# Cross-attention on one Trainium2 core: eleven block products of 64 rows in place of twelve for the folded key weights

## The chip, the cores and the metric

The kernel runs on one core of one Trainium2 chip. The metric is the device time of one execution in microseconds. A core has PE (TensorE, matrix products into the banks of PSUM), DVE (VectorE), ACT (ScalarE), POOL (GpSimd) and SP (SyncE, which here issues the transfers). Each engine works through its own queue in order; semaphores order work between engines.

## The reference

Multi-head cross-attention, all in float32, with 16 batches of 256 queries (256 wide), 77 keys (192 wide) and 8 heads of width 256:

```python
Q = (img_embed @ Wq).reshape(B, -1, H, D).transpose(0, 2, 1, 3)
K = (sent_embed @ Wk).reshape(B, -1, H, D).transpose(0, 2, 1, 3)
V = (sent_embed @ Wv).reshape(B, -1, H, D).transpose(0, 2, 1, 3)
score = jnp.einsum('bhqd,bhkd->bhqk', Q, K) / math.sqrt(D)
score = jnp.where(mask, score, -jnp.inf)
attn = jax.nn.softmax(score, axis=-1)
ctx = jnp.einsum('bhqk,bhkd->bqhd', attn, V).reshape(B, -1, H * D)
out = ctx @ Wo + img_embed
mu = jnp.mean(out, axis=-1, keepdims=True)
var = jnp.var(out, axis=-1, keepdims=True)
return (out - mu) * jax.lax.rsqrt(var + EPS) * gamma + beta
```

## The kernel before

The weights are folded. For each head, G = Wk Wq^T / sqrt(D) is a 192 x 256 matrix, kept as gA (the first 128 of its 192 rows, per head) and gB (the other 64; two heads share the partitions). With the transposed keys c, kept as cA (128 rows) and cB (64 rows, there twice), A = G^T c is a 256 x 77 matrix for each batch and head, and the scores are x A. In the same way U = Wv Wo (uA, uB) gives vw = c U, and the output is p vw.

The prologue builds G and U, and A of group 0 (a group is four batches). After it a loop runs over b from -1 to 14. One pass does, in the order of the code:

- `scores` of the two query tiles of batch b+1 on PE (L303, into ps), `shift` of them on DVE (L320: adds the mask and takes the largest score of a row), `exponential` on ACT (L340), `weigh` (the reciprocal on DVE, L355, then the product p on POOL, L361), and `turn` (the transpose pT of p on DVE, L371);
- `prepare_vw` on PE (L227 for the 128 rows, L238 for the 64; bank pv, copied to vw by ACT at L963), and `differences` on POOL (L414, ts);
- `prepare_a`: A of two heads of a later group, a quarter of a group's A, as 308 columns (four batches of 77 keys) for each head and half of the 256 rows: L193 for the 128 rows with 32 columns of weights each, L205 for the 64 rows; four banks pa, copied to a by ACT (L963);
- `seven` on PE (L450: p vw of batch b by seven block products; banks pm and po), `sums` on POOL (L431 to L434, ss, for the next `seven`), `add_product` on DVE (L498, po into xg), `add_seven` on POOL (L484);
- the normalisation of batch b-1: `finish` (L506, L509), `spread` on ACT (L527, L528), `normalise` on DVE (L548, L577); `turn_last` (L293) and `transpose_x` (L165) on DVE.

Every second pass (b = -1, 1, 3, 5, ...) is a long one: it holds `prepare_vw` for two batches and two quarters of A. The passes between are short and hold neither. Until b = 7 the quarters are those of groups 1, 2 and the first half of group 3.

All PSUM tiles come from one pool of 8 banks, taken in turn: a tile waits until the tile eight places before it has been read by all its readers. A long and a short pass take 24 banks. The order on each engine is the order in which the code records the operations; nothing reorders them. Transfers of x, c and the outputs go through SP's queue.

Of the kernel before, what the change touches and what calls it, by code (L numbers as in the profile page):

```python
# [27 lines left out]
def kernel(  # L28
# [52 lines left out]
    gB = const.tile([P, NF, DI], F32, tag="gB", name="gB")  # L81

# [85 lines left out]
    def prepare_a(g, places, lo=0, hi=GB, rest_first=False):  # L168
# [16 lines left out]
        def cols(dc, i):  # L185
            return slice((2 * i + dc) * BK, (2 * i + dc + 1) * BK)
# [29 lines left out]
        return part_A, part_B, copies  # L216

# [382 lines left out]
    with tc.tile_pool(name="wonce", bufs=1) as wp:  # L600
# [33 lines left out]
        def turn_rest():  # L634
            nc.vector.transpose(flat(cA)[:, rest], flat(cA)[:, rest])
            nc.gpsimd.tensor_copy(cRA, cA[:, :, KM:])

        def turn_rest_last():
            nc.vector.transpose(flat(cB)[LB:, rest], flat(cB)[LB:, rest])
            nc.gpsimd.tensor_copy(flat(cB)[:LB, rest], flat(cB)[LB:, rest])  # L640
            nc.gpsimd.tensor_copy(cRB, cB[:, :, KM:])
# [186 lines left out]
        def g_of_pair(a):  # L828

            banks = [ps_mm.tile([P, DI], F32, tag="mm", name=f"pgb_{a}_{e}") for e in range(2)]  # L830
            for n in range(4):
                for i in range(2):
                    for e in range(2):
                        nc.tensor.matmul(  # L834
                            banks[e][half(i)],
                            kT_blk[a][half(e), n, half(i)],
                            qT_blk[a][half(e), n],
                            start=(n == 0),
                            stop=(n == 3),
                        )  # L840
            for e, o in enumerate(banks):
                nc.scalar.mul(gA[:, 2 * a + e], o, D ** -0.5)
# [42 lines left out]
        for a in range(1, NF):  # L885
# [7 lines left out]
            a_of_pairs(a, rest_first=True)  # L893
        load_x(0)
# [10 lines left out]
        for j in range(NF // 2):  # L905
# [13 lines left out]
            for e, pw in enumerate(  # L919
# [3 lines left out]
                for i in range(2):  # L923
                    for k in range(2):
# [24 lines left out]

    def work_of(b, rest_first=False):  # L950
        g, n = b // GB + 1, b % GB
        work = [prepare_vw(b, rest_first)]
        if g < NG - 1 or g == NG - 1 and n < NF // 2:
            work.append(prepare_a(g, (n,), rest_first=rest_first))
        elif b <= NS:
# [21 lines left out]
    for b in range(-1, B - 1):  # L977
# [17 lines left out]
        works = work_of(b + 1) if alone or n % 2 == 0 else []  # L995
        for part_A, _, _ in works:
            part_A()
        for _, part_B, _ in works:
            part_B()
# [23 lines left out]
        ahead = works and not alone  # L1023
        if old and not ahead:
            spread(old[0], old[-1] + 1)
        if ahead:
            copy_out(works)
            if old:
                spread(old[0], old[-1] + 1)
            works = work_of(b + 2, rest_first=True)  # L1030
            for _, part_B, _ in works:
                part_B()
            for part_A, _, _ in works:
                part_A()
        copy_out(works)
# [4 lines left out]
        if b < NS:  # L1040
            if now:
                seven(b)
            if old:
                invert(old[0], old[-1] + 1)
                normalise(old[0])
            for t in new:
                turn(t)
            if b < 0:
                for t in range(QT, GT, 2):
                    transpose_x(t)  # L1050
                bias_of(GB, B)
            if alone or ahead:
# [65 lines left out]
```

## Time and profile before

| | us |
|---|---|
| median of 3 runs | 270.32 (270.11 to 270.44) |
| the profiled execution | 269.95 |
| its span | 268.2 |
| PE busy | 262.5 (98%) |
| DVE busy | 185.9 (69%) |
| POOL busy | 173.2 (65%) |
| ACT busy | 157.6 (59%) |
| A by L193 and L205 (PE, all groups) | 36.6 and 20.4 |

The span is the profiler's time from the first to the last instruction; the device time has 1.75 us around it. The clock granted to PE is 1.00 throughout. A row of a group gives line, engine, operation, out<-in, shapes and count, then the busy time, the mean duration of one in ns, and the idle time of the engine just before such instructions with what ended it. A row of the timeline gives start, length, engine, line and operation; idle time before it stands in brackets. A float32 matmul leaves two records on PE.

### The profile page before, as it was taken

To read this page: it belongs to the slowest core of one execution; us is meant where nothing else is said; L and a number is where in the kernel's file an instruction comes from. 1 tells how busy PE (TensorE), PEld (TensorE's weight loads), DVE (VectorE), ACT (ScalarE), POOL (GpSimd) and SP (SyncE) were. 2 spreads that over 40 slices of the span, in tenths; PEclk is the share of its full clock that TensorE was granted. 3 is DMA by queue.
4 is the path that set the end of the run, shared out by engine and by line. 5 is a ranking of instruction groups with operands and counts; after the bars stand their busy time and mean duration, and the time that the engine had idled before them with its cause. 6 is when DMAs were issued, how large, how long until landed. Compare 5 with 4: busy or idle time off the path is not lost.

```text
span 268.2 us, 14455 instructions
## 1 busy us (share of the span) xinstructions
PE 262.5 (98%) x6090; PEld 191.8 (72%) x6090; DVE 185.9 (69%) x808; ACT 157.6 (59%) x667; POOL 173.2 (65%) x240
## 2 busy tenths in 40 slices
PE   8999999999999999999999999999999999999992
PEld 8566578944984699459944995499669957985662
DVE  1555967493583868665886379647977887799785
ACT  3243336536857565955596468737775595636772
POOL 1042005728399739994799669965998799585452
PEclk9999999999999999999999999999999999999999
DMA  6989987901500130232012401340034010100112
GB/s 190 217 199 228 334 138 142 311 21 34 129 7 2 46 80 2 63 111 71 5 43 90 112 5 43 91 113 2 6 120 122 4 45 2 44 22 22 46 40 80
DMA packets 41696, 22.69 MB, mean 85 GB/s; under 512 B 24144, under 2 KB 40608, under 8 KB 41632
## 3 DMA queue, kind: packets, MB, share of 16 engines
q1 hardware_dynamic: 41248, 20.98, 30.1%
q0 software_dynamic: 384, 0.79, 1.3%
q8 instruction: 48, 0.79, 1.3%
q14 instruction: 16, 0.13, 0.2%
HBM read 17.57 MB, written 4.19 MB: 81 GB/s over the span
## 4 chain that ended last, share of the span: by engine, by line
PE 98%; DVE 1%; issue 0%; DVEq 0%
PE ps L303 25%; PE pa L193 13%; PE pv L227 11%; PE po L450 11%; PE pm L450 8%; PE pa L205 6%; PE pv L238 6%; PE po L383 4%; PE pu L773 3%; PE pr L263 2%; PE pgb L834 2%; PE pw L787 1%; PE idle L703 1%; PE pr L274 1%; PE phb L850 1%; PE po L399 1%
## 5 line engine op out<-in xcount | busy, mean ns | idle before, releaser
L340 ACT ACTIVATE s<-s,top 128x77 f32<-128x77 f32 x256 | 85.3, 346 | 44.2 <-DVE top L320 37.9
L303 PE MATMUL ps<-a,xT 128*32 128x154 f32 x2048 | 69.9, 294 | 0.0
L303 PEld LDWEIGHTS ps<-a,xT 128*32 128x32 f32 x2048 | 66.2, 110 | 1.2 <-issue 0.4
L361 POOL TENSOR_TENSOR p<-s,rden 128x512 f32<-128x512 f32 x64 | 47.5, 768 | 29.5 <-DVE rden L355 29.4
L320 DVE CUSTOM_DVE_ANT_0 s<-ps,bias 128x77 f32<-128x77 f32 x256 | 43.5, 232 | 14.3 <-PE ps L303 14.3
L340 ACT ACTIVATION_READ_ACCUMULATOR s<-s,top 128x1 f32 x224 | 42.0, 187 | 0.0
L193 PE MATMUL pa<-cA,gA 128*32 128x308 f32 (+1 forms) x576 | 36.6, 395 | 0.0
L193 PEld LDWEIGHTS pa<-cA,gA 128*32 128x32 f32 x576 | 18.3, 110 | 21.0 <-issue 7.0
L484 POOL TENSOR_TENSOR xg<-xg,m 128x256 f32<-128x256 f32 x39 | 28.7, 736 | 6.6 <-DVE xg L498 4.5
L577 DVE SCALAR_TENSOR_TENSOR xg<-xg,rstd,bet 128x256 f32<-128x256 f32 x27 | 22.9, 847 | 14.0 <-ACT rstd L528 12.6
L227 PE MATMUL pv<-uA,cA 128*32 128x512 f32 x256 | 30.6, 595 | 0.0
L371 DVE STREAM_TRANSPOSE pT<-p 128x640 f32<-128x640 f32 x32 | 25.5, 821 | 3.4 <-POOL p L361 3.3
L414 POOL TENSOR_TENSOR ts<-vw 128x768 f32<-128x768 f32 x13 | 24.0, 1848 | 5.9 <-ACT vw L963 5.9
L963 ACT COPY vw<-pv 128x512 f32<-128x512 f32 x32 | 17.8, 584 | 14.8 <-PE pv L227 8.3
L498 DVE TENSOR_TENSOR xg<-po,xg 128x256 f32<-128x256 f32 x31 | 11.5, 405 | 13.8 <-PE po L450 13.3
L320 DVE DVE_READ_ACCUMULATOR2_ANT top<- 128x1 f32 x256 | 20.8, 81 | 0.0
L205 PE MATMUL pa<-cB,gB 64*32 64x308 f32 (+2 forms) x512 | 20.4, 387 | 0.0
L963 ACT COPY a<-pa 128x308 f32<-128x308 f32 (+1 forms) x56 | 18.9, 395 | 1.9 <-PE pa L193 0.4
L205 PEld LDWEIGHTS pa<-cB,gB 64*32 64x32 f32 (+1 forms) x512 | 11.0, 110 | 11.4 <-issue 6.2
L548 DVE SCALAR_TENSOR_TENSOR xg<-xg,mv,gam 128x256 f32<-128x256 f32 x30 | 17.6, 588 | 0.1
L238 PE MATMUL pv<-uB,cB 64*32 64x512 f32 x256 | 17.3, 597 | 0.0
L227 PEld LDWEIGHTS pv<-uA,cA 128*32 128x32 f32 x256 | 7.5, 109 | 12.8 <-issue 9.9
(119 smaller groups left out, 404.1 us busy)
## 6 DMA issues: line engine op xcount, KB each, us to landing
xg<-in_x_dram SPq DMA_DIRECT2D x8, 512.0 KB, 4.4
xT<-in_x_dram SPq DMA_DIRECT2D x56, 64.0 KB, 2.6
out_dram<-xg SPq DMA_DIRECT2D x11, 256.0 KB, 2.2
wo<-in_L_xattn_Wo_dram SPq DMA_DIRECT2D x4, 512.0 KB, 7.8
wq_blk<-in_L_xattn_Wq_dram SPq DMA_DIRECT2D x12, 128.0 KB, 4.3
out_dram<-xg SPq DMA_DIRECT2D x10, 128.0 KB, 1.9
wk_blk<-in_L_xattn_Wk_dram SPq DMA_DIRECT2D x12, 96.0 KB, 3.6
wvT<-in_L_xattn_Wv_dram POOLq DMA_DIRECT2D x8, 96.0 KB, 6.6
```

The source lines that it names most:

```text
L193: nc.tensor.matmul(flat(o[i * BK : (i + 1) * BK]), gA[:, h, cols(dc, i)], flat(cA[:, batches, :]), start=not rest_first and n in opening, ...
L205: nc.tensor.matmul(flat(banks[j + k][i * BK : (i + wide) * BK]), gB[half(k), h // 2, dc * P + i * BK : dc * P + (i + wide) * BK], flat(cB[ ...
L227: nc.tensor.matmul(pv[k][i * BK : (i + 1) * BK], cA[:, b, k * BK : (k + 1) * BK], uA[:, parts, :, i], start=not rest_first, stop=rest_first,)
L238: nc.tensor.matmul(pv[k][i * BK : (i + 1) * BK], cB[half(k), b, k * BK : (k + 1) * BK], uB[half(k), parts, :, i], start=rest_first, stop=n ...
L303: nc.tensor.matmul(ps[m // 2][i * BK : (i + 1) * BK, m % 2 * 2 * S2 : (m % 2 + 1) * 2 * S2], xT_of[t // PT][:, j * NM + m, dc], flat(a_of[ ...
L320: nc.vector.tensor_tensor_reduce(s[:, h], ps[a][:, k * S2 : (k + 1) * S2], bias[:, b, :], scale=-1.0, scalar=FAR, op0=ALU.add, op1=ALU.min ...
L340: nc.scalar.activation(s[:, h], s[:, h], AF.Exp, bias=top[:, one], scale=-1.0, accum_out=den[:, one] if summed_by_act(t) else None,)
L361: nc.gpsimd.tensor_tensor(part, e_mh[:, :, :, keys], rden_mh.unsqueeze(3).to_broadcast(list(part.shape)), ALU.mult,)
L371: nc.vector.transpose(pT_of[t].rearrange("p n m q -> p m n q"), p.rearrange("p m (n k) -> p m n k", k=BK),)
L450: nc.tensor.matmul(out[i * BK : (i + 1) * BK], weight[:, i], moving, start=first and n == 0, stop=final and n == len(terms) - 1,)
L484: nc.gpsimd.tensor_tensor(to, to, what, ALU.add)
L963: nc.scalar.copy(dst, src)
```

## The change

For groups 1, 2 and the first half of group 3 the three block rows of G (64 rows each) and the two halves of a group's batches (154 columns) are combined as in a fast matrix product. For one head, A's two halves of 128 rows and the two halves of the batches are four outputs, each a sum of three block products: twelve. Five products (`middle`) and six (`outer`) of sums of the blocks now give them: eleven.

On PE, `prepare_fast(g, u)` takes the place of a quarter of `prepare_a`. Its matmuls contract 64 rows into 64 rows of PSUM. `products` walks eleven pairs; a pair has one product on partitions 0 to 63 and one on 64 to 127, each in two halves of 64 output rows, so four matmuls of 154 columns. The two heads use four banks: mids and ends for each. The first product of `middle` goes to a bank alone and is copied to a by ScalarE (L369 of the changed kernel), before the same bank is started anew by that head's second product of `middle`, in the fifth pair for the first head and in the eighth for the second.

On DVE, `put_together(e)` makes a of one head from its two banks and that copy by four additions (L372).

The operands need sums: `sums_of_g`, `last_sums_of_g` (gS, and gC, a copy of half of gB on the other partitions), `sums_of_c` (cT) and `differences_of_c` (cD). They run once, in the prologue, on POOL and, as copies, on ACT. The copies of `turn_rest` and `turn_rest_last` go from POOL to ACT. gA's columns are stored in another order, so that 64 of them are adjacent.

In the long passes up to b = 7 the vw products of both batches now come first, then the two calls of `products`, and the sums of DVE stand between and behind the two transposes of p. The core of the diff:

```diff
+    add, subtract = (
+        partial(nc.gpsimd.tensor_tensor, op=op) for op in (ALU.add, ALU.subtract)
+    )
...
+    def sums_of_g():
+        for parts, sums, e, own, other in parts_of_g():
+            nc.scalar.copy(sums[own, 0, e], parts[other, 1, e])
+            nc.scalar.copy(gC[own], gB[other, :, P:])
+        for parts, sums, e, own, other in parts_of_g():
+            s1, s2, s3 = (sums[own, n, e] for n in range(3))
+            add(s1, s1, parts[own, 1, e])
+            subtract(s2, s1, parts[own, 0, e])
+            subtract(s3, parts[own, 0, e], parts[own, 1, e])
...
+    def sums_of_c(lo, hi):
+        xs, ys = halves_of(cA, lo, hi)
+        t1, t2, t3, t4 = (cT[:, n, lo - 1 : hi - 1] for n in range(4))
+        subtract(t1, ys, xs)
+        for own, other in ((low, high), (high, low)):
+            nc.gpsimd.tensor_copy(t2[own], ys[other])
+        subtract(t3, t2, ys)
+        subtract(t2, t2, t1)
+        for own, other in ((low, high), (high, low)):
+            nc.gpsimd.tensor_copy(t4[own], t2[other])
+        subtract(t4, xs, t4)
...
+        def middle(e):
+            h, own = heads[e], (high, low)[e]
+            return [
+                ((mids[e], 2), from_g(own, h, 0), c_of(cA, own, xs)),
+                ((mids[e], 0), from_s(own, 0, h), t_of(own, 0)),
+                ((mids[e], 2), from_s(own, 1, h), t_of(own, 1)),
+                ((mids[e], 1), from_s(own, 2, h), t_of(own, 2)),
+                ((mids[e], 1), lambda i: gC[own, u, half(i)], c_of(cB, own, ys)),
+            ]
...
+        def pairs():
+            o, m = outer(0), middle(1)
+            ones = o[:2] + m[:1] + o[2:] + m[1:]
+            o, m = outer(1), middle(0)
+            return list(zip(ones, m[:1] + o[:3] + m[1:] + o[3:]))
+
+        def products():
...
+                for i in range(2):
+                    for ((bank, n), weight, moving), (start, stop, _) in zip(pair, flags):
+                        nc.tensor.matmul(
+                            bank[half(i), n], weight(i), moving, start=start, stop=stop,
+                        )
+                for ((bank, n), _, _), (_, _, one) in zip(pair, flags):
+                    if one:
+                        nc.scalar.copy(blocks[lone[id(bank)]][:, 0], by_batch(bank)[:, n])
...
+        def put_together(e):
+            mid, end, of = by_batch(mids[e]), by_batch(ends[e]), blocks[e]
+            plus(of[:, 3], mid[:, 2], of[:, 0])
+            plus(of[:, 1:3], mid[:, 0:2], of[:, 3:4].to_broadcast([P, 2, HB, S2]))
+            plus(of[:, 3], mid[:, 0], of[:, 2])
+            plus(of[:, 0:3], end, of[:, 0:3])
...
         def turn_rest():
             nc.vector.transpose(flat(cA)[:, rest], flat(cA)[:, rest])
-            nc.gpsimd.tensor_copy(cRA, cA[:, :, KM:])
+            nc.scalar.copy(cRA, cA[:, :, KM:])
 
         def turn_rest_last():
             nc.vector.transpose(flat(cB)[LB:, rest], flat(cB)[LB:, rest])
-            nc.gpsimd.tensor_copy(flat(cB)[:LB, rest], flat(cB)[LB:, rest])
-            nc.gpsimd.tensor_copy(cRB, cB[:, :, KM:])
+            nc.scalar.copy(flat(cB)[:LB, rest], flat(cB)[LB:, rest])
+            nc.scalar.copy(cRB, cB[:, :, KM:])
...
+        if quick:
+            works += work_of(b + 2)
+            for part_A, *_ in works:
+                part_A()
+            for _, part_B, _ in works:
+                part_B()
+            copy_out(works[:1])
+            products, put_together = prepare_fast(g, n)
+            products()
+            copy_out(works[1:])
...
+            next_products, next_together = prepare_fast(g, n + 1)
+            next_products()
+            if old:
+                spread(old[0], old[-1] + 1)
...
+            if quick:
+                if b >= 0:
+                    turn(new[0])
+                put_together(0)
+                put_together(1)
+                if b >= 0:
+                    turn(new[1])
             if old:
                 invert(old[0], old[-1] + 1)
                 normalise(old[0])
-            for t in new:
-                turn(t)
...
+            if quick:
+                next_together(0)
+                next_together(1)
```

How this moves the queues is shown for the long pass b = 3, whose tiles of queries are 8 and 9. DVE's queue from the second reciprocal to the next shift, before (pT is the transpose of p; xg holds the rows to be normalised; po is the result of `seven`):

```order
L355 RECIPROCAL rden_9_1933<-den_9_1921 128x8
L548 SCALAR_TENSOR_TENSOR xg_1_518<-xg_1_518,mv_0_1346,gam_69 128x256
L577 SCALAR_TENSOR_TENSOR xg_1_518<-xg_1_518,rstd_4_1944,bet_90 128x256
L371 STREAM_TRANSPOSE pT_8_2086<-p_0_85 128x4x5x32
L371 STREAM_TRANSPOSE pT_9_2088<-p_1_86 128x4x5x32
L165 STREAM_TRANSPOSE xT_3_1441<-xT_3_1441 128x512 x2
L548 SCALAR_TENSOR_TENSOR xg_1_518<-xg_1_518,mv_0_1346,gam_69 128x256
L577 SCALAR_TENSOR_TENSOR xg_1_518<-xg_1_518,rstd_4_1944,bet_90 128x256
L498 TENSOR_TENSOR xg_1_518<-po_3_2017,xg_1_518 128x256 x2
```

And after, from the same reciprocal through the first two heads (pf is a bank of `prepare_fast`; two more heads, eight rows of the same kind, follow the row with rstd, and then the transposes of x):

```order
L520 RECIPROCAL rden_9_1987<-den_9_1975 128x8
L536 STREAM_TRANSPOSE pT_8_2211<-p_0_88 128x4x5x32
L372 TENSOR_TENSOR a_2_2028<-pf_2_0_0_2029,a_2_2028 128x2x77
L372 TENSOR_TENSOR a_2_2028<-pf_2_0_0_2029,a_2_2028 128x4x77
L372 TENSOR_TENSOR a_2_2028<-pf_2_0_0_2029,a_2_2028 128x2x77
L372 TENSOR_TENSOR a_2_2028<-pf_2_0_0_2030,a_2_2028 128x6x77
L372 TENSOR_TENSOR a_2_2028<-pf_2_1_1_2031,a_2_2028 128x2x77
L372 TENSOR_TENSOR a_2_2028<-pf_2_1_1_2031,a_2_2028 128x4x77
L372 TENSOR_TENSOR a_2_2028<-pf_2_1_1_2031,a_2_2028 128x2x77
L372 TENSOR_TENSOR a_2_2028<-pf_2_1_1_2032,a_2_2028 128x6x77
L536 STREAM_TRANSPOSE pT_9_2221<-p_1_89 128x4x5x32
L713 SCALAR_TENSOR_TENSOR xg_1_532<-xg_1_532,mv_0_1365,gam_69 128x256
```

Sixteen additions have come into the queue, eight of them between the two transposes of p, and the first transpose now stands ahead of the normalisation. ACT's queue of the same pass behind the exponentials, before:

```order
L963 COPY vw_4_1849<-pv_4_0_1850 128x4x128
L963 COPY vw_4_1849<-pv_4_1_1851 128x4x128
L963 COPY a_2_1852<-pa_2_0_0_0_1853 128x4x77
L963 COPY a_2_1852<-pa_2_1_0_0_1854 128x4x77
L963 COPY a_2_1852<-pa_2_0_1_0_1855 128x4x77
L963 COPY a_2_1852<-pa_2_1_1_0_1856 128x4x77
```

And after, down to the logarithm of the normalisation:

```order
L1136 COPY vw_4_1956<-pv_4_0_1957 128x4x128
L1136 COPY vw_4_1956<-pv_4_1_1958 128x4x128
L369 COPY a_2_2028<-pf_2_0_0_2029 128x2x77
L369 COPY a_2_2028<-pf_2_1_1_2031 128x2x77
L1136 COPY vw_5_1991<-pv_5_0_1992 128x4x128
L1136 COPY vw_5_1991<-pv_5_1_1993 128x4x128
L369 COPY a_2_2028<-pf_2_2_0_2081 128x2x77
L369 COPY a_2_2028<-pf_2_3_1_2083 128x2x77
L692 ACTIVATE log_4_2131<-mv_0_1365,eps_75 128x2
```

The eight copies of A have become four of half the width, and the logarithm stands behind all of them. Last, ACT's queue in the prologue after the change, between the last copies of U and the first exponentials of tiles 0 and 1:

```order
L1092 COPY uB_83<-pw_1_0_644 64x8x32 x4
L252 COPY gS_519<-gS_519 64x4x128 x2
L801 COPY cRA_86<-cA_84 128x208
L805 COPY cB_85<-cB_85 64x896
L806 COPY cRB_87<-cB_85 128x208
L505 ACTIVATE s_0_744,den_0_777<-s_0_744,top_0_745 128x77 x8
L505 ACTIVATE s_1_754,den_1_790<-s_1_754,top_1_755 128x77 x8
L142 COPY vr_812<-pr_0_814 128x2x16x13
```

Before, the exponentials followed the copies of U at once; now five copies stand between, three of which stood in POOL's queue.

More of the change, by code (lines that the diff above doesn't have):

```diff
@@ new lines, in last_sums_of_g, with halves_of @@
+    def last_sums_of_g():
+        for parts, sums, e, own, other in parts_of_g():
+            nc.scalar.copy(sums[other, 0, e], sums[own, 1, e])
+        for parts, sums, e, own, other in parts_of_g():
+            subtract(sums[other, 0, e], parts[other, 0, e], sums[other, 0, e])
+    def halves_of(c, lo, hi):
+        groups = c[:, lo * GB : hi * GB].rearrange("p (g y b) k -> p y g (b k)", y=2, b=HB)
+        return groups[:, 0], groups[:, 1]
+    def sums_of_c(lo, hi):
[9 more added lines that the diff above has]
+        subtract(t4, xs, t4)
@@ L934 @@
         turn_rest_last()
+        sums_of_c(1, 2)
         sum_of(uB)
@@ L947, with fast @@
     pools[1] = vwp = late
+    def fast(b):
+        return b < B - GB - GB // 2
     def work_of(b, rest_first=False):
@@ L952, in work_of @@
         work = [prepare_vw(b, rest_first)]
-        if g < NG - 1 or g == NG - 1 and n < NF // 2:
-            work.append(prepare_a(g, (n,), rest_first=rest_first))
-        elif b <= NS:
+        if b <= NS and not fast(b):
             part = (0, 2) if g < NG else (2, GB)
@@ L994 @@
         alone = b + 1 >= B - GB // 2
[L995 to L999, printed above, removed]
+        ahead = not alone and n % 2 == 0
+        quick = ahead and fast(b + 1)
+        works = work_of(b + 1) if alone or ahead else []
+        if not quick:
+            for part_A, *_ in works:
+                part_A()
+            for _, part_B, _ in works:
+                part_B()
         if b == B - 2:
@@ L1022 @@
             weigh(t)
[L1023 to L1027, printed above, removed]
+        if quick:
+            works += work_of(b + 2)
+            for part_A, *_ in works:
+                part_A()
+            for _, part_B, _ in works:
+                part_B()
+            copy_out(works[:1])
+            products, put_together = prepare_fast(g, n)
+            products()
+            copy_out(works[1:])
+        elif not alone or old:
+            if ahead:
+                copy_out(works)
             if old:
                 spread(old[0], old[-1] + 1)
[L1030 to L1035, printed above, removed]
+            if ahead:
+                works = work_of(b + 2, rest_first=True)
+                for _, part_B, _ in works:
+                    part_B()
+                for part_A, *_ in works:
+                    part_A()
+        if not quick:
+            copy_out(works)
+        if quick:
+            if b < 0:
+                for t in new:
+                    turn(t)
+                for t in range(QT, GT, 2):
+                    transpose_x(t)
+            next_products, next_together = prepare_fast(g, n + 1)
+            next_products()
+            if old:
+                spread(old[0], old[-1] + 1)
         if b + 1 < NS:
@@ L1045 @@
                 normalise(old[0])
-            for t in new:
-                turn(t)
             if b < 0:
-                for t in range(QT, GT, 2):
-                    transpose_x(t)
                 bias_of(GB, B)
+            elif not quick:
+                for t in new:
+                    turn(t)
+            if quick:
+                next_together(0)
+                next_together(1)
             if alone or ahead:
```

85 lines of the change are left out of this document (82 added, 3 removed).

## The prediction

> **What bounds the kernel now.** I read the page first, then PE's timeline, then the busy time by stage, and last the timelines of DVE, ACT and POOL around one stage of the loop.
>
> ```profile
> PE 262.5 (98%) x6090; PEld 191.8 (72%) x6090; DVE 185.9 (69%) x808; ACT 157.6 (59%) x667; POOL 173.2 (65%) x240
> PE 98%; DVE 1%; issue 0%; DVEq 0%
> ```
>
> The second line is the chain that ended last: PE nearly from end to end. A saved PE microsecond is a saved microsecond as long as nothing new makes PE wait. PE's timeline (start, length, engine, line, operation) for two long passes (b=1 from 74.81, b=3 from 102.70):
>
> ```profile
> 74.81 4.37 PE L303 MATMUL ps<-a,xT 128*32 128x154 f32 x128
> ...
> 102.70 4.37 PE L303 MATMUL ps<-a,xT 128*32 128x154 f32 x128
> 106.88 1.90 PE L227 MATMUL pv<-uA,cA 128*32 128x512 f32 x16
> 108.60 2.26 PE L193 MATMUL pa<-cA,gA 128*32 128x308 f32 x32
> 110.79 1.09 PE L238 MATMUL pv<-uB,cB 64*32 64x512 f32 x16
> 111.67 1.24 PE L205 MATMUL pa<-cB,gB 64*32 64x308 f32 x32
> ...
> 118.55 0.62 PE L450 MATMUL pm<-vw,pT 128*32 128x128 f32 x16
> ```
>
> A long pass and the short one behind it repeat every 102.70-74.81 = 27.89 us. Next, how full the other engines are in the short pass (first row) and the long one (second). Columns: PE, PEld, DVE, ACT, POOL busy (instructions), clock, DMA share, GB/s.
>
> ```profile
> 94.59:102.70 8.11, 8.11 (x265) 7.74 (x261) 6.05 (x43) 6.44 (x35) 3.83 (x6) 1.00 0.17 37
> 102.70:122.47 19.77, 19.77 (x456) 12.48 (x451) 13.14 (x54) 11.73 (x48) 18.41 (x24) 1.00 0.28 79
> ```
>
> DVE has 27.88-19.19 = 8.7 us free in a period. How much of that an in-order queue can use is the question of this change:
>
> ```profile
> 95.89 0.24 DVE L320 CUSTOM_DVE_ANT_0 s<-ps,bias 128x77 f32<-128x77 f32 x1 [0.29 <-PE ps L303]
> ...
> 104.27 0.85 DVE L371 STREAM_TRANSPOSE pT<-p 128x640 f32<-128x640 f32 x1 [0.52 <-POOL p L361]
> 105.04 0.72 DVE L498 TENSOR_TENSOR xg<-po,xg 128x256 f32<-128x256 f32 x2
> 105.68 0.22 DVE L320 CUSTOM_DVE_ANT_0 s<-ps,bias 128x77 f32<-128x77 f32 x1
> ...
> 108.21 0.55 DVE L548 SCALAR_TENSOR_TENSOR xg<-xg,mv,gam 128x256 f32<-128x256 f32 x1
> 108.79 0.84 DVE L577 SCALAR_TENSOR_TENSOR xg<-xg,rstd,bet 128x256 f32<-128x256 f32 x1
> 109.55 0.70 DVE L293 STREAM_TRANSPOSE vr<-vr 128x512 f32<-128x512 f32 x1
> ...
> 111.65 0.20 DVE L355 RECIPROCAL rden<-den 128x8 f32<-128x8 f32 x1 [0.27 <-ACT s L340]
> ...
> 115.35 1.56 DVE L371 STREAM_TRANSPOSE pT<-p 128x640 f32<-128x640 f32 x2
> 116.83 1.26 DVE L165 STREAM_TRANSPOSE xT<-xT 128x512 f32<-128x512 f32 x2
> ...
> 122.72 0.42 DVE L498 TENSOR_TENSOR xg<-po,xg 128x256 f32<-128x256 f32 x1 [3.38 <-PE po L450]
> ```
>
> In brackets: idle time before a row and what ended it. Only the last one is real reserve, DVE waiting for PE. The others are latency: shift, exponential, reciprocal, product by 1/den, transpose, each on another engine. The other ends of that loop, ACT and then POOL:
>
> ```profile
> 106.01 0.36 ACT L340 ACTIVATE s<-s,top 128x77 f32<-128x77 f32 x1 [3.29 <-POOL ts L414]
> ...
> 111.97 1.07 ACT L963 COPY vw<-pv 128x512 f32<-128x512 f32 x2 [0.35 <-PE pv L238]
> ...
> 104.20 1.82 POOL L414 TENSOR_TENSOR ts<-vw 128x768 f32<-128x768 f32 x1
> ...
> 112.76 2.89 POOL L361 TENSOR_TENSOR p<-s,rden 128x512 f32<-128x512 f32 x4
> ```
>
> Call x the start of shift on DVE. In the long pass x = 105.68. ACT's first exponential starts at x+0.33 and the second reciprocal, which waits for the last one, at x+5.97. POOL works without a gap from 104.20 and reaches its product p at x+7.08.
>
> **PE's gain.** In b=3 the stage from 106.88 to 118.55 takes 11.67; two vw products take 2 x ((108.60-106.88)+(111.67-110.79)) = 5.20, so the two quarters of A take 6.47. After the change each quarter is 11 pairs, each pair a group of four 64x64 tiles, 154 columns. The rate of such groups is in the prologue (64 records are 32 matmuls or 8 groups, since a float32 matmul leaves two records):
>
> ```profile
> 31.33 3.68 PE L773 MATMUL pu<-wo,wv_turned 64*64 64x256 f32 x64
> 34.82 1.92 PE L787 MATMUL pw<-wo,wv_turned 64*64 64x256 f32 x32
> ```
>
> (34.82-31.33)/8 = 0.436 us for 256 columns, 0.262 for 154. Two quarters: 22 x 0.262 = 5.77. The work now goes from 32-column to 64x64 tiles and back, one change of shape more; from the spread of the stages I put 0.2 to 0.3 on it. Gain 0.4 to 0.5 in each of five long passes, 2.2 us in all, if PE never waits. The Trainium skill, "TensorEngine Tiling (Array Packing)", section Key Properties, says that a change of tiling mode drains the TensorE. That agrees in kind with the allowance; no row here isolates it.
>
> **What DVE must do for it.** For each head put_together is four sums of 154, 308, 154 and 462 elements per partition with one operand in PSUM, each needing the one before. Rows near them:
>
> ```profile
> L498 DVE TENSOR_TENSOR xg<-po,xg 128x256 f32<-128x256 f32 x31 | 11.5, 405 | 13.8 <-PE po L450 13.3 <-PE po L383 0.5
> L913 DVE COPY uA<-pu 128x512 f32<-128x512 f32 x1 | 0.7, 692 | 1.2 <-PE pu L773 1.2
> L963 ACT COPY a<-pa 128x154 f32<-128x154 f32 x16 | 3.5, 292 | 0.4 <-PE pa L193 0.4
> ```
>
> From 405 ns at 256 and 692 at 512 the slope is 1.12 ns an element: 0.29, 0.46, 0.29, 0.64, sum 1.68, with small gaps between dependent instructions 1.75 us. The lower end is the stride of independent ones (105.04 to 105.68: two in 0.64, so 0.32 for 256 elements): 0.20+0.38+0.20+0.55 = 1.3. The upper end, 1.95, is with 0.1 of handover for two of the waits. I take 1.75, since each of the four waits for its predecessor. Four heads: 7.0 us on DVE in each long pass, in four consecutive periods after the first one in the prologue. ACT in turn loses eight 308-element copies and gets four of 0.29; that is a gain on an engine that isn't the bound.
>
> **DVE's queue in the new order**, from x: the second reciprocal at x+5.97, as now, since the exponentials set it. Then the first turn waits for POOL: 7.08 + 2.89/2 = x+8.55, and 0.75 long (two in 116.83-115.35 = 1.48): 9.3. put_together of two heads: 12.8. Second turn: 13.55. normalise 1.1 (109.55-108.21 = 1.34 at its slowest): 14.65. Two more heads: 18.15. Transposes of x 1.26: 19.4. normalise: 20.65. The two sums po, 0.64: the next shift starts at x+21.3. In the short pass the same walk takes 105.68-95.89 = 9.79 now; without the idle time that PE's scores put between its shifts 9.2, no less, because the second reciprocal is still 5.97 behind shift and p and the second turn follow it. Period: 21.3+9.2 = 30.5, and PE has only 27.89-0.45 of work in it. So I expect DVE's loop, not PE, to set these passes: 2.6 us late in each against the old clock. On average DVE still has free time; it lies in waits that can't be filled, since what stands behind a waiting turn is held too.
>
> **Where PE feels it.** The lone product of middle() must be copied by ScalarE before its bank is reused by the fifth pair. That copy stands on ACT behind 16 exponentials and two vw copies: x+5.97+1.07+0.29 and handovers = x+7.5. PE reaches the fifth pair 4.18 (scores) + 5.2 + four pairs = 10.4 after the start of its scores. In b=3 x is 2.98 after it, so the copy comes at 10.5: no slack at all. Any lateness of DVE becomes a wait of PE in the same pass. The Trainium skill, "TensorEngine Tiling (Array Packing)", section PSUM Bottleneck, warns that tiling speeds up TensorE but not the emptying of PSUM, which may then become the bottleneck. Here the array gains one product in twelve while VectorE gets all the emptying; by that rule the change is a loss, which is where my rows lead as well.
>
> **Entry.** The copies of turn_rest and turn_rest_last go from POOL to ACT, ahead of the first exponentials:
>
> ```profile
> 45.19 0.36 ACT L340 ACTIVATE s<-s,top 128x77 f32<-128x77 f32 x1 [1.73 <-DVE top L320]
> ...
> 47.56 1.11 DVE L639 STREAM_TRANSPOSE cB<-cB 64x896 f32<-64x896 f32 x1
> ...
> 54.06 1.80 ACT L133 COPY vr<-pr 128x416 f32<-128x416 f32 x4 [3.28 <-PE pr L274]
> ...
> 58.97 1.85 DVE L165 STREAM_TRANSPOSE xT<-xT 128x512 f32<-128x512 f32 x3
> ...
> 66.71 4.37 PE L303 MATMUL ps<-a,xT 128*32 128x154 f32 x128
> ...
> 68.00 0.24 DVE L320 CUSTOM_DVE_ANT_0 s<-ps,bias 128x77 f32<-128x77 f32 x1 [5.50 <-PE ps L303]
> ...
> L902 POOL TENSOR_TENSOR uA<-uA 128x512 f32<-128x512 f32 x1 | 1.3, 1272 | 0.0
> L636 POOL COPY cRA<-cA 128x208 f32<-128x208 f32 x1 | 0.4, 358 | 0.9 <-DVE cA L635 0.9
> ```
>
> The copy of cB (896 elements, 0.9 by ACT's rows) must follow the transpose that ends at 48.67, and the exponentials follow it: 50.0 instead of 45.19. They take 5.6, so ACT's vr copies begin at 55.7 instead of 54.06, and DVE's, behind the second reciprocal and a memset, at 56.5. POOL's added work (25 sums and copies of 154 to 512 elements, some 20 us by the last two rows) fills its idle time up to 60 us and makes ss of batch 0 a little late; I put the wait for it at 1 to 2 us, parallel to DVE's lateness. On DVE the transposes end near 63.2; then come two heads, the bias (1.75) and two heads: shift of batch 1 starts near 72.5. It starts at 68.00 now, 1.3 after the scores of 66.71. A short pass without old rows (9.1) puts x of b=1 at 81.6. PE's fifth pair then runs at 89.1 instead of 74.81+10.4 = 85.2: 3.9 late. Bounds: 2.1 with heads of 1.3, 5.3 with heads of 1.95.
>
> **Sum.** 3.9 at entry, 3 x 2.6 = 7.8 up to b=7, minus 0.6 (PE is shorter behind the fifth pair), plus 0.6 (in b=9 the bank of po comes late once more): +11.7. The profiled execution took 269.95 (span 268.2), against a median of 270.32; 269.95+11.7 = 281.65, forecast 281.5.
>
> Its own range: heads of 1.3 give a period of 28.7 and 2.1+2.4-0.6 = +3.9, 273.9; heads of 1.95 and the short pass at 9.79 give 31.9 and 5.3+12+0 = +17.3, 287.
>
> **Rivals.**
> - Faster: DVE's sums stay hidden and PE keeps its 2.2: 267.7. For it speak DVE's mean of 69% and the 3.38 us wait at 122.72. It needs a period below 27.4, so heads below about 1 us, or a POOL that reaches p 2.4 earlier together with heads of 1.5. It is decided at the fifth pair of b=3: if no wait stands there, this one holds.
> - A small loss, 270.9 to 274: dependent sums overlap as independent ones do. Against it: centre (0.55 from 108.21) and scale (from 108.79), where one needs the other, don't overlap.
> - Worse still: PE's clock. It is 1.00 in both windows above, in which PE never idles. A stall of nearly 3 us in each period is new. If the matmuls after three such stalls ran at half speed for as long as the stall, that costs 3 x 1.5 and more: 286 to 291. The Trainium skill, "TensorE: Matmul & The Clock Gate", section HAM oscillation, has PE throttled again by idle gaps above about 3.4 us; by that rule my stalls stay just short of it, and no run here shows such a gap.
> - The 64x64 groups don't run four at a time, so that the change isn't a saving on PE: 5.8 more in each long pass, near 299. The 0.436 us of L773 speaks clearly against it.
>
> **Numbers.** A difference of 0.2% (0.5 us) is about what can be told from no change. Forecast (DVE's loop sets the period, 274 to 287) 0.74; small loss below it 0.08; faster 0.12; no change by chance 0.02; clock or beyond 287, 0.04. The range leaves out faster, no change and the top: 271.5 to 287. Faster 0.12, same 0.02, slower 0.86.
>
> **What would show it.** Right: idle time of PE before the products of prepare_fast, ended by ACT, 1.5 to 4 us in each long pass; starts of the scores 30.5 apart up to b=7 and 27.9-like spacing after; DVE above 90% busy between 80 and 190 us, with its waits for POOL p and ACT; the first exponential near 50; pairs of 0.26. Wrong: PE at 98% again (then the sums are hidden), a head on DVE under 1.3 us, or PE waiting for seven's ss on POOL rather than for ACT.

## The result, and the profile after

| | us |
|---|---|
| before, median of 4 runs on the same chip | 270.38 (270.11 to 270.80) |
| after, median of 4 runs | 282.06 (281.64 to 283.73) |
| ratio | 1.0442 [1.0398, 1.0486] |
| the profiled execution of after, and its span | 283.73, 281.9 |

The kernel is 4.4% slower; the forecast was 281.5. The page of the changed kernel: busy time of the engines, the chain that ended last, and the clock granted to PE in 40 slices.

```profile
PE 266.7 (95%) x6330; PEld 207.5 (74%) x6330; DVE 217.2 (77%) x888; ACT 151.1 (54%) x656; POOL 189.5 (67%) x262
PE 36%; DVE 15%; ACT 13%; issue 1%; DVEq 0%; ACTq 0%
PEclk9999999999999999979999999989999999999999
```

PE was 98% of the chain before; now it has 36% of the span, and DVE and ACT stand in it. Still no engine but PE is above 77% busy: the new bound can't be seen in the shares. It shows in what PE waits for (sum, times, longest) and in PE's timeline at the fifth pair of the four quarters that wait:

```profile
PE pf L360 <- ACT a L369: 6.2, 4, 2.4
PE pm L615 <- POOL ss L598: 1.7, 1, 1.7
PE pv L392 <- ACT vr L142: 1.2, 1, 1.2
```

```profile
89.72 0.34 PE L360 MATMUL pf<-cT,gS 64*64 64x154 f32 x1 [0.46 <-ACT a L369]
...
120.14 0.34 PE L360 MATMUL pf<-cT,gS 64*64 64x154 f32 x1 [2.36 <-ACT a L369]
...
150.84 0.34 PE L360 MATMUL pf<-cT,gS 64*64 64x154 f32 x1 [0.98 <-ACT a L369]
...
181.27 0.34 PE L360 MATMUL pf<-cT,gS 64*64 64x154 f32 x1 [2.38 <-ACT a L369]
```

These starts are 30.42, 30.70 and 30.43 us apart, against 27.89 for the same work before: (181.27-89.72) - 3 x 27.89 = 7.9 us lost in three periods. ScalarE's copy is the last link that PE sees, but not the slow one. DVE's timeline in the long pass b=3, whose shift starts at x = 113.03:

```profile
120.99 0.85 DVE L536 STREAM_TRANSPOSE pT<-p 128x640 f32<-128x640 f32 x1 [1.74 <-POOL p L526]
122.01 3.70 DVE L372 TENSOR_TENSOR a<-pf,a 128x154 f32<-128x154 f32 x8 [0.17 <-PE pf L360]
125.62 0.83 DVE L536 STREAM_TRANSPOSE pT<-p 128x640 f32<-128x640 f32 x1
126.38 0.45 DVE L713 SCALAR_TENSOR_TENSOR xg<-xg,mv,gam 128x256 f32<-128x256 f32 x1
126.93 0.77 DVE L742 SCALAR_TENSOR_TENSOR xg<-xg,rstd,bet 128x256 f32<-128x256 f32 x1
127.63 3.68 DVE L372 TENSOR_TENSOR a<-pf,a 128x154 f32<-128x154 f32 x8
131.22 1.30 DVE L174 STREAM_TRANSPOSE xT<-xT 128x512 f32<-128x512 f32 x2
132.44 0.45 DVE L713 SCALAR_TENSOR_TENSOR xg<-xg,mv,gam 128x256 f32<-128x256 f32 x1
132.92 0.48 DVE L742 SCALAR_TENSOR_TENSOR xg<-xg,rstd,bet 128x256 f32<-128x256 f32 x1
133.32 0.75 DVE L663 TENSOR_TENSOR xg<-po,xg 128x256 f32<-128x256 f32 x2
```

From the first transpose of p to the next shift at 133.98 DVE has one gap, 0.17 us. In the kernel before, 3.38 us of waiting for PE stood there. A row of eight sums (two heads) takes 3.7 us, so the four heads 7.4. What is left of DVE's free time stands ahead of that stretch, in waits for POOL's p (1.74) and for ACT's exponentials, and cannot be reached by what is queued behind.

### The profile page after: what moved, and what is told of

Same layout as the page of the kernel before. It is cut to its first block, busy times and chain, and to the rows that moved or that the text cites. A ratio compares the mean times of both kernels' runs of the same rounds, so it can differ in the third digit from the quotient of the medians.

```text
span 281.9 us, 15074 instructions
## 1 busy us (share of the span) xinstructions
PE 266.7 (95%) x6330; PEld 207.5 (74%) x6330; DVE 217.2 (77%) x888; ACT 151.1 (54%) x656; POOL 189.5 (67%) x262
## 4 chain that ended last, share of the span: by engine, by line
PE 36%; DVE 15%; ACT 13%; issue 1%; DVEq 0%; ACTq 0%
ACT s L505 12%; PE ps L468 10%; DVE a L372 5%; PE po L615 5%; PE pf L360 4%; PE po L548 4%; PE pm L615 4%; PE pv L392 4%; DVE xg L742 3%; DVE pT L536 2%; PE pv L403 2%; PE pa L202 1%; DVE xg L663 1%; DVE xT L174 1%; DVE xg L713 1%
## 5 line engine op out<-in xcount | busy, mean ns | idle before, releaser
L485 DVE CUSTOM_DVE_ANT_0 s<-ps,bias 128x77 f32<-128x77 f32 x256 | 42.1, 231 | 1.8 <-PE ps L468 1.8
L372 DVE TENSOR_TENSOR a<-pf,a 128x154 f32<-128x154 f32 x80 | 34.0, 436 | 3.9 <-PE pf L360 1.2
L392 PE MATMUL pv<-uA,cA 128*32 128x512 f32 x256 | 29.6, 593 | 1.2 <-ACT vr L142 1.2
L360 PE MATMUL pf<-cT,gS 64*64 64x154 f32 x240 | 19.3, 308 | 6.2 <-ACT a L369 6.2
L520 DVE RECIPROCAL rden<-den 128x8 f32<-128x8 f32 x32 | 6.1, 191 | 20.7 <-ACT s L505 20.5
L360 PEld LDWEIGHTS pf<-cT,gS 64*64 64x64 f32 x240 | 16.6, 139 | 7.3 <-ACT a L369 7.3
L392 PEld LDWEIGHTS pv<-uA,cA 128*32 128x32 f32 x256 | 8.4, 110 | 14.2 <-issue 9.5
L360 PE MATMUL pf<-cB,gB 64*64 64x154 f32 x160 | 17.9, 310 | 0.0
L713 DVE SCALAR_TENSOR_TENSOR xg<-xg,mv,gam 128x256 f32<-128x256 f32 x30 | 17.2, 574 | 0.1
L596 POOL TENSOR_TENSOR ss<-pT 128x256 f32<-128x256 f32 x13 | 11.0, 847 | 8.9 <-DVE pT L536 8.9
L403 PE MATMUL pv<-uB,cB 64*32 64x512 f32 x256 | 16.3, 597 | 0.0
```

What stands on the lines that cost most here:

```text
L360: nc.tensor.matmul(bank[half(i), n], weight(i), moving, start=start, stop=stop,)
L372: nc.vector.tensor_tensor(out, *of, ALU.add)
L392: nc.tensor.matmul(pv[k][i * BK : (i + 1) * BK], cA[:, b, k * BK : (k + 1) * BK], uA[:, parts, :, i], start=not rest_first, stop=rest_first,)
L485: nc.vector.tensor_tensor_reduce(s[:, h], ps[a][:, k * S2 : (k + 1) * S2], bias[:, b, :], scale=-1.0, scalar=FAR, op0=ALU.add, op1=ALU.min ...
```

## The experiments

Times are medians; "ratio" is against the kernel before, measured beside each experiment, with medians of 270.4 to 270.7 us.

### e1: half of DVE's sums

Of the four sums of put_together, one of 154 and one of 308 elements are kept. The other two are left out, and with them a part of A's value:

```diff
-            plus(of[:, 1:3], mid[:, 0:2], of[:, 3:4].to_broadcast([P, 2, HB, S2]))
-            plus(of[:, 3], mid[:, 0], of[:, 2])
-            plus(of[:, 0:3], end, of[:, 0:3])
+            plus(of[:, 1:3], end[:, 0:2], of[:, 0:1].to_broadcast([P, 2, HB, S2]))
```

> put_together keeps two of its four sums (154 and 308 elements, one on each bank); the other two are left out, and with them part of A's value. PE, ACT and POOL do what they did. DVE theory (the in-order loop of DVE sets the passes): a head costs 0.8 us in place of 1.83, a long pass 3.1 in place of 7.3, the loop falls from 30.5 to 26.3 us, below PE's 27.4, and PE's waits ahead of the fifth pair go from b = 3 on. What stays is the entry (1.2 us for vr, 1.7 for ss) less PE's gain of some 2: 269.5 to 273. Copy theory (the place of the lone copy in ACT's queue is the cost by itself): the waits stay, 279 or more.

Measured: 270.71 us, ratio 1.0014 [0.9991, 1.0036]. All of the loss goes with the sums, though PE does the same products as in after. It also shows what the eleven products are worth when PE is free to run. PE's timeline of e1 in b=3:

```profile
103.51 4.37 PE L466 MATMUL ps<-a,xT 128*32 128x154 f32 x128
107.70 3.62 PE L390 MATMUL pv<-uA,cA 128*32 128x512 f32 x32
111.25 1.95 PE L401 MATMUL pv<-uB,cB 64*32 64x512 f32 x32
113.12 0.49 PE L360 MATMUL pf<-cA,gA 64*64 64x154 f32 x8
...
119.05 0.64 PE L613 MATMUL pm<-vw,pT 128*32 128x128 f32 x16
...
122.99 4.37 PE L466 MATMUL ps<-a,xT 128*32 128x154 f32 x128
```

The two quarters take 119.05-113.12 = 5.93 (6.47 before by the same kind of reading), but the vw products ahead of them 113.12-107.70 = 5.42 (5.20 before). The pass is 122.99-103.51 = 19.48, against 19.77: the gain is 0.29 us, not 0.4 to 0.5. That size rests on b=1 (19.49) and b=3. In b=5 and b=7 of this execution, at 272.18 us the second slowest of ten, PE stood idle for 0.86 and 0.15 us with no releaser in the trace, and the passes took 20.80 and 20.09; why stays open.

### e6: one more sum

Each head gets a fifth sum of 462 elements, into a spare tile: `plus(by_batch(spare), mid, of[:, 0:3])`.

> One more sum of 462 elements per head on DVE, into a tile that nobody reads. DVE theory: 0.67 us a head, 2.7 in each long pass, three periods and the entry: 10 to 11 us more, 289 to 296. If DVE had room and PE, ACT or the clock set the pace: within 2 us of the changed kernel.

Measured: 299.11 us, ratio 1.1049 [1.1018, 1.1080]. The sign is as expected, the size 3 us above the top of the range. Fifth pairs stand 33.97 us apart (125.35, 159.32, 193.30): 3.4 more than after, where four sums of 0.64 with their gaps make 2.7. The rest shows in b=3, in the windows behind PE's stall (the granted clock is the third number from the end) and in DVE's timeline:

```profile
125.35:127.50 2.15, 2.15 (x36) 2.07 (x40) 0.84 (x1) 1.09 (x3) 2.15 (x5) 0.50 0.63 149
127.50:129.00 1.50, 1.50 (x44) 1.48 (x40) 1.12 (x3) 0.00 (x0) 1.50 (x1) 0.78 0.39 136
```

```profile
126.15 0.84 DVE L538 STREAM_TRANSPOSE pT<-p 128x640 f32<-128x640 f32 x1 [1.72 <-POOL p L528]
...
127.80 1.86 DVE L373 TENSOR_TENSOR a<-pf,a 128x154 f32<-128x154 f32 x4 [0.81 <-PE pf L361]
```

After a stall of 2.49 us PE resumes at half clock, and DVE waits 0.81 us for the products (0.80 in b=5 and b=7): 2.7 + 0.8 is the measured 3.4 to 0.1. In after the same wait is 0.17. Here the clock seems to enter the loop; no run with this fifth sum and a full clock was made.

### e3: the products before the wait reordered

Rival: what counts is the chain over ScalarE's copy. All six outer products go ahead of the second product of middle, so that PE reaches the first head's reused bank three pairs later, in the eighth pair (the second head's stood there already, and its lone product now comes first):

```diff
-            ones = o[:2] + m[:1] + o[2:] + m[1:]
+            ones = m[:1] + o + m[1:]
...
-            return list(zip(ones, m[:1] + o[:3] + m[1:] + o[3:]))
+            return list(zip(ones, m[:1] + o + m[1:]))
```

> The same eleven pairs in another order: the lone products first, then the six of outer, then the other four of middle, so that the bank with the copy is needed in the eighth pair for both heads and no more in the fifth. DVE theory: PE's wait moves to the eighth pair and is 0.8 us shorter, but the period stays near 30.5, since put_together needs the same last pairs: 280 to 283. Copy theory: each of the four waits gets 0.8 us shorter and the time with it: 277 to 279.5.

Measured: 282.85 us, ratio 1.0447 [1.0408, 1.0485]. PE still waits 5.8 us for the copy (6.2 in after): what it gained by coming to it later, DVE's lateness took again. The place of the reused bank in PE's order doesn't matter.

### e8: the waits filled with products

Rival: PE's own time or its clock. Eight matmuls of zeros stand ahead of the fifth pair in b = 3, 5 and 7:

```diff
+                for _ in range(filled if k == 4 else 0):
+                    nc.tensor.matmul(ends[0][:, 0, :P], fill, fill, start=False, stop=False)
...
-            products()
+            products(8 if b >= 3 else 0)
```

> Eight matmuls of zeros (128x128, some 0.23 us each) ahead of the fifth pair of the first quarter in b = 3, 5 and 7: 1.9 us of PE work in each, 5.6 in all, which adds zero to a bank. DVE theory: PE would have waited there, so nothing is longer; the clock no longer falls behind the wait, which may give back 1 to 2 us: 280 to 282.5. If PE's own work counted in these passes: 286 to 288.

Measured: 281.98 us, ratio 1.0421 [1.0399, 1.0443], as after. PE's waits at the fifth pairs fall to 1.1 us, its mean clock rises to 1.000, and the period stays (fifth pairs 30.4 apart). More work for PE costs nothing, and a full clock gains nothing that the medians show.

### e4 and e2: the entry

In e4 ScalarE's copies of cB and cRB stand behind the first exponentials instead of ahead of them. e2 keeps the whole new prologue (POOL's sums, ScalarE's copies) with the loop of the kernel before.

> ACT's copies of cB and cRB (1.3 us and a wait for DVE's transpose) go behind the first exponentials. The exponentials of tiles 0 and 1 then start near 45.8 and not 50.5, and PE's wait for vr (1.15 us) goes. DVE theory: this takes 1 to 2 us off the entry and nothing off the period: 280 to 281. If the entry were the main cause: 276 or less.

> The kernel before with all of the change's prologue (gA in the new order, gS, gC, cT, cD, the copies on ACT), and the loop of before: the sums are made and not used. DVE theory: only the wait for vr stays, since the sums of put_together are not there to make the bias and ss late: 1 to 2.5 us over the kernel before, 271 to 273. If the entry were the main cause: 276 or more.

Measured: e4 281.52 us, ratio 1.0412 [1.0389, 1.0436], a little above its range; e2 271.55 us, ratio 1.0037 [1.0023, 1.0052]. PE's first wait in e2, and its scores of batch 0, which were at 66.71 before:

```profile
56.11 1.92 PE L392 MATMUL pv<-uA,cA 128*32 128x512 f32 x16 [1.15 <-ACT vr L142]
67.80 4.37 PE L468 MATMUL ps<-a,xT 128*32 128x154 f32 x128
```

The new prologue by itself costs 1.0 us, by this one wait. e4 takes that wait away. Its median is 0.5 us below that of after; in its trace the fifth pairs of b=1 and b=3 start 0.94 and 0.95 us earlier than there (88.78 and 119.19), and the period stays at 30.4. The entry is a part that adds once; it isn't what sets the period.

### e7: the wait for POOL filled

If the length of DVE's walk is the bound, work moved into its wait for p must shorten the period. In the long passes the first normalisation of the old rows goes there, and ScalarE's log and rstd for it go ahead of the copies of vw:

```diff
+            if old:
+                spread(old[0], old[-1] + 1)
             copy_out(works[:1])
...
-            if old:
-                spread(old[0], old[-1] + 1)
...
             if quick:
+                if old:
+                    invert(old[0], old[-1] + 1)
+                    normalise(old[0])
                 if b >= 0:
                     turn(new[0])
...
-            if old:
+            elif old:
                 invert(old[0], old[-1] + 1)
                 normalise(old[0])
```

> The changed kernel with one piece of DVE's loop moved: in the long passes the first normalisation of the old rows (two instructions, 1.1 to 1.3 us) stands ahead of the first transpose of p, where DVE waits 1.75 us for POOL, and not behind both transposes; ScalarE's two small operations for it (log and rstd, 0.5 us) stand ahead of the copies of vw. Nothing is left out. DVE's loop as the bound: 1.1 to 1.3 us less in the period of each of the passes at b=1, 3, 5 and 7, fifth pairs 29.2 to 29.4 us apart in place of 30.4 to 30.7, against 0.5 us once because the lone copy comes later on ScalarE: 278.0 to 280.0 us. If what bounds is PE's own products or the chain over ScalarE's copy (exponentials, vw copies, lone copy): 282 to 284 us, since that chain gets 0.5 longer in each pass. If POOL's p is the bound: unchanged, 281.5 to 282.5.

Measured: 279.83 us, ratio 1.0335 [1.0307, 1.0364]: 2.2 us less than after, by moving two DVE instructions and two of ScalarE. DVE's timeline of e7 in b=3:

```profile
119.18 1.08 DVE L742 SCALAR_TENSOR_TENSOR xg<-xg,rstd,bet 128x256 f32<-128x256 f32 x1
120.52 0.85 DVE L536 STREAM_TRANSPOSE pT<-p 128x640 f32<-128x640 f32 x1 [0.26 <-POOL p L526]
```

The wait is 0.26 in place of 1.74, and shifts of the long passes start 29.54, 29.98 and 29.74 apart (82.67, 112.21, 142.19, 171.93). That is 0.7 to 0.9 less per period, under the 1.1 to 1.3 that I expected: the walk behind the first turn lost the 1.25 of the normalisation (126.38 to 127.63 above), but POOL's p, and with it the first turn, came at x+8.31 in place of x+7.96.

### e5, e9, e10: half the dose

If a long pass has no room for 7.4 us of sums, it may have room for 3.7. In e5 only the second quarter of each long pass is made by eleven products, last on PE, the first by twelve as before.

> Of the two quarters of A in a long pass only the second goes by eleven products, behind both vw products and the other quarter; its sums on DVE stand last ahead of po, the sums of the prologue are made for its heads alone, and cB's copies are back on POOL. DVE theory: 3.7 us more on DVE in a long pass, a loop near 27, just below PE's 27.6, and PE gains 0.25 in each of five: 268.5 to 270.3. If the eleven products cost PE more in waits and changes of shape than they save: 271 or more.

Measured: 271.78 us, ratio 1.0056 [1.0040, 1.0072]: a miss. PE waits for nothing that the waits list, and yet its long passes are 19.92, 20.27, 19.92 and 19.92 (before 19.78). ACT's and PE's timelines in b=3:

```profile
115.15 1.34 ACT L1141 COPY a<-pa 128x308 f32<-128x308 f32 x4
116.38 0.31 ACT L694 ACTIVATE log<-mv,eps 128x2 f32<-128x2 f32 x1
116.72 0.20 ACT L695 ACTIVATE rstd<-log 128x2 f32<-128x2 f32 x1
116.83 0.46 ACT L371 COPY a<-pf 128x154 f32<-128x154 f32 x2
```

```profile
116.64 0.42 PE L362 MATMUL pf<-cB,gB 64*64 64x154 f32 x2
117.15 0.34 PE L362 MATMUL pf<-cT,gS 64*64 64x154 f32 x1
```

The two rows of PE are one pair. Its first product starts on time, its second 0.51 us later, behind the lone copy, which I had left behind four copies of a. (In b=1, b=5 and b=7 the same step is 0.17, and the passes are shorter by as much; my next expectation took the 0.51 for all of them.) A stall of half a pair is covered by the modelled end of the other half (0.42) and so is no idle time in the list. e9 puts the lone copies ahead of two of those copies and of the log:

```diff
-            copy_out(first)
-            if old:
-                spread(old[0], old[-1] + 1)
+            copy_out(first[:1])
+            of_a = [copy for _, _, copies in first[1:] for copy in copies()]
+            for copy in of_a[:2]:
+                nc.scalar.copy(*copy)
             next_products, next_together = prepare_fast(g, n + 1)
             next_products()
+            if old:
+                spread(old[0], old[-1] + 1)
+            for copy in of_a[2:]:
+                nc.scalar.copy(*copy)
```

> The kernel with every second quarter by eleven products (e5), with one order changed: on ScalarE the lone copies stand behind the first two copies of a, and no longer behind all four and the log and rstd. In e5's trace the fifth pair's second product begins 0.51 us behind its first (88.27 or 116.64 to 117.15), and the lone copy on ScalarE runs from 116.83. If that wait is where e5's saving went: long passes of 19.35 to 19.5 us in place of 19.92 (before: 19.78), five of them, so 2.1 to 2.5 us off e5: 269.2 to 269.8 us, ratio to before 0.995 to 0.998. If the eleven products with their changes of tile shape cost PE as much as the twelve: 271.3 to 272 as e5.

Measured: 271.78 us, ratio 1.0042 [1.0024, 1.0059]: the pair no longer splits and the first three long passes are 19.71, 19.77 and 19.71, but the fourth is 21.05: 0.83 us of the 1.3 more lie at L202, where PE waited for DVE (from there to the next vw products 2.90 in place of 2.07). What was late next was ScalarE's rstd, on which DVE waited 1.95 us in b=3 and 2.51 in b=5. e10 moves spread ahead of the copies of vw, and changes nothing else.

> The kernel with every second quarter by eleven products and early lone copies (e9), with ScalarE's log and rstd for the old rows moved from behind the lone copies to ahead of the copies of vw. In e9's trace the fifth pair no longer waits and the first three long passes are 19.71, 19.77 and 19.71 us (before 19.78), but DVE waits 1.95 to 2.5 us for rstd in each long pass, starts its shifts 2.9 us later than before (108.58 against 105.68), and at b=7 PE waits for it: that long pass is 21.05 us. If DVE's lateness is what spoils e9: shifts within 1 us of those before, all long passes 19.6 to 19.8 us, no idle time of PE in the loop, and 269.5 to 270.5 us, ratio 0.996 to 1.000: no more than equal to before, since one quarter by eleven products saves PE under 0.1 us in a pass. If it isn't: 271.3 to 272.2 as e9 and e5.

Measured: 269.95 us (269.56 to 270.58), ratio 0.9975 [0.9966, 0.9984]: a quarter of a per cent faster than before. Its chain that ended last, and PE's scores of b=3 and b=4:

```profile
PE 95%; DMA 2%; SPq 1%; DVE 1%; issue 0%; DVEq 0%
```

```profile
103.21 4.37 PE L470 MATMUL ps<-a,xT 128*32 128x154 f32 x128
...
122.92 4.37 PE L470 MATMUL ps<-a,xT 128*32 128x154 f32 x128
```

PE is the chain again, and each long pass up to b=7 is 19.71 or 19.72.

### e11: the control

The kernel before with e10's early spread alone:

```diff
-        if old and not ahead:
+        if old:
             spread(old[0], old[-1] + 1)
         if ahead:
             copy_out(works)
-            if old:
-                spread(old[0], old[-1] + 1)
```

> A control for e10: the kernel before, all quarters by twelve products, with only e10's last order: ScalarE's log and rstd for the old rows ahead of the copies of vw in the long passes. e10 was faster than before by 0.25%, and its long passes are 19.71 against 19.78 us. If that gain belongs to the eleven products: this kernel equals before (269.9 to 270.8 us, ratio 0.999 to 1.001), since PE never waits for DVE in it and DVE's wait for rstd (2.57 us in each long pass) is covered; long passes stay 19.78. If the early rstd alone brings it: 269.6 to 270.0 us, ratio 0.996 to 0.9985.

Measured: 270.68 us, ratio 1.0008 [0.9996, 1.0021]. In a kernel whose PE never waits the early rstd gains nothing, so e10's gain doesn't come from that order alone. Its size isn't fully accounted for: 0.07 us in each of the four passes timed here is 0.28 of the 0.71 between the medians, and e10's profiled execution, at 270.58 the slowest of its runs and 0.6 later at b=1 than that of before, doesn't show the rest.

## Why the prediction was right, step by step

**The bound.** Shown. Take sums away and the loss goes (e1), add some and it grows by more than they cost (e6), shorten DVE's walk by order alone and it shrinks (e7); reorder PE's products (e3) or add to them (e8) and nothing moves. Of the signs I had named, the first exponential near 50, pairs of 0.26 and idle time ended by ACT came. Three did not come as I gave them. The scores of the long passes start 28.5 to 32.1 us apart, 30.4 in the mean. Only two of the four waits were 1.5 us or more; the others were 0.46 and 0.98. And DVE was busy for 91.2 of the 110 us from 80 to 190, which is 83% and not above 90%: its waits inside the loop count as idle.

**The walk.** The total held better than its parts. I had the first turn at x+8.55; it is at x+7.96, as POOL's p comes earlier. Four heads take 7.4 where I had 7.0: the sums alone are as the rows said, the handovers are more. The groups of put_together by shape (busy time, mean ns of one, then idle time before them):

```profile
L372 DVE TENSOR_TENSOR a<-pf,a 128x462 f32<-128x462 f32 x20 | 12.8, 640 | 1.4
L372 DVE TENSOR_TENSOR a<-pf,a 128x154 f32<-128x154 f32 x40 | 12.5, 312 | 1.8 <-PE pf L360 1.2
L372 DVE TENSOR_TENSOR a<-pf,a 128x308 f32<-128x308 f32 x20 | 9.6, 479 | 0.7
```

0.312+0.479+0.312+0.640 = 1.74 against my 1.68, and 3.7/2 = 1.85 with gaps. The long pass is 133.98-113.03 = 20.95 (I had 21.3) and the short one behind it 143.74-133.98 = 9.76. Here a step failed: I had taken 0.6 off the short pass, on the ground that it no longer waits for PE's scores, and it kept the 9.79 of before. The second reciprocal of the short pass, before (x = 95.89) and after (x = 133.98):

```profile
101.86 0.20 DVE L355 RECIPROCAL rden<-den 128x8 f32<-128x8 f32 x1 [0.37 <-ACT s L340]
139.94 0.20 DVE L520 RECIPROCAL rden<-den 128x8 f32<-128x8 f32 x1 [1.60 <-ACT s L505]
```

It stands at x+5.97 and x+5.96, since the exponentials set it: the time saved in the shifts was only waited off there. The two errors cancel, 30.7 against 30.5, so that a part of the agreement is luck.

**PE's gain.** The term was mis-sized: 0.29 us per long pass (e1) for the 0.4 to 0.5 I took. The pairs run at 0.262 as the prologue's groups said, and beginning and ending them costs 0.16, less than the 0.2 to 0.3 I had put on it. What the sum left out is the vw products: once they stand together, they take 5.42 for 5.20; my 5.20 came from rows where the quarters stood between them. At 0.29 a pass, a twelfth less work would be worth 1.5 us in five passes, and the new prologue takes 1.0 of it (e2). The 0.5 left over isn't seen in e1, whose executions spread from 269.80 to 272.35. The Trainium skill, "TensorEngine Tiling (Array Packing)", section Key Properties, says that a change of tiling mode drains the TensorE; the 0.16 agrees in kind.

**Entry and the waits.** The exponentials start at 50.4 (I had 50.0), the shift of batch 1 at 73.52 (72.5), that of b=1 at 82.59 (81.6), the fifth pair at 89.72 (89.1). The wait for ss is 1.7 (1 to 2), once. All are 0.4 to 1 us later than forecast; four heads, each 0.1 longer than I had them, make 0.4 of it. The entry thus costs 89.72 - 85.2 = 4.5 us in place of 3.9.

**The end.** I had put -0.6 behind the fifth pair of b=7 and +0.6 for b=9. In the profiled execution this stretch cost about +1.1 instead: scores of b=8 at 191.76, against 178.24 before, are 13.5 late where the fifth pair at 181.27 was 12.4 late. This is the clock, below: in e4, where it stays at 1.00, the same stretch is 188.81 - 179.99 = 8.8 us, against 191.76 - 181.27 = 10.5 in after and 178.24 - (85.2 + 3 x 27.89) = 9.4 before, so that the -0.6 was right for a full clock. The other three runs, at 281.64 to 282.17, lie lower by about what the clock costs here; they have no trace. The b=9 pass is 17.2 us in e4 and 16.7 in after, where it was 16.7 before: 0.4 or nothing for the +0.6.

**The rivals.** "Faster" failed where it was said to be decided, at the fifth pair of b=3. "A small loss" failed with the heads: dependent sums don't overlap. The 64x64 groups do run four at a time (e1).

**The clock** is the rival I judged wrongly in its premise and rightly in its weight. PE's windows around the stall of b=3 in after, and then behind the stall at the same place in e4:

```profile
120.00:121.00 1.00, 0.86 (x24) 0.87 (x28) 0.01 (x1) 1.00 (x4) 1.00 (x3) 0.89 0.51 43
121.00:124.00 3.00, 3.00 (x55) 3.00 (x51) 2.73 (x6) 0.24 (x2) 3.00 (x4) 0.50 0.49 166
124.00:125.00 1.00, 1.00 (x32) 1.00 (x28) 0.90 (x3) 0.58 (x3) 0.09 (x2) 0.90 0.00 0
```

```profile
119.19 0.34 PE L360 MATMUL pf<-cT,gS 64*64 64x154 f32 x1 [2.35 <-ACT a L369]
119.19:123.19 4.00, 4.00 (x124) 4.00 (x128) 3.02 (x7) 2.06 (x7) 3.96 (x6) 1.00 0.56 135
```

In after PE idled 2.36 us and the clock then stood at 0.50 for 3.4 us. The Trainium skill, "TensorE: Matmul & The Clock Gate", section HAM oscillation, names idle gaps above about 3.4 us; I concluded that mine stay short of it. The trace does not agree: stalls of 2.36 and 2.38 us, of 2.49 in e6 and of 1.82 in e7 (b=3) were enough. But the length doesn't decide alone: the three stalls of 2.34 and 2.35 us in e4 left the clock at 1.00. What the traces show beside it is a grid. A mean clock of 0.89 in 120:121 can be read as 0.22 us at 0.50, so that the slow stretch starts at 120.78. Read in this way, after's two stretches start at 120.78 and 182.22, which is 18 x 3.413 us apart, and e6's five at 76.95, 124.74, 158.87, 193.00 and 220.31, which is 14, 10, 10 and 8 times 3.413; each of them, like the one in e3 and the one in e7, lasts 3.41 to 3.42 us. So it seems to matter where a stall lies between two points of such a grid. No run moves a stall on purpose, so that this is not shown as the cause.

The clock cost little because DVE was late anyhow: half speed for 3.4 us only used up the lead PE would have waited off. Two runs say so. e8 has no such stall at the fifth pairs, and e4 has the stalls with the clock at 1.00; both keep a period of 30.4 us. It costs where DVE catches up with PE's products (probably the 0.81 us in e6's b=3), or where no later wait swallows it (the end of after's profiled execution, about 1.7 us).

## What to carry to other kernels

Price added work on an in-order engine in its loop, from one wait to the next, and not by its mean load: a 69% busy DVE had 8.7 us free per period, and of the 7.4 us added it could take up 4.8 before the period grew (by 30.5 - 27.9 = 2.6). When a faster way of computing moves work to another engine, try a smaller dose before dropping it, and first reorder the small operations that the second engine waits for: half the quarters, with ScalarE's copies and rstd early, turned +4.4% into -0.25%. And a stall need not be in the list of waits: compare the starts of the same pass between kernels.

## What the runs showed of the hardware

Stalls of PE of 1.82 to 2.49 us were followed by a granted clock of 0.50 for 3.41 to 3.42 us in after, e6, e7 and e3, and three stalls of 2.34 and 2.35 us in e4 and three of 1.94 and 1.95 in e3 were not. The slow stretches of one execution start whole multiples of 3.413 us apart (after, e6); they began up to about a microsecond after PE had resumed (after, 182.22 against 181.27) or while it still stood (e6, 124.74 against 125.35). A quarter of A in groups of 64x64 tiles cost 0.262 us per pair of products from the fourth pair on, and about 0.16 us more for the two quarters at their beginning and end. Dependent DVE sums with one operand in PSUM and 154, 308 and 462 elements took 312, 479 and 640 ns.
